# Three-layer graph convolution on one core: where layer 1's gathers and the next layer's loads are issued, bfloat16 keys, degrees by diagonal matrices

## The chip, the cores and the metric

The kernel runs on one core of a Trainium2 chip. The metric is the time of one execution on the device, in microseconds, as the median of three runs; lower is better. Beside those runs there is one execution under the hardware profiler, from which every duration below comes.

## The reference

N = 2500 nodes with 256 features, E = 80000 directed edges (src, dst), sorted by dst. After a layer norm and a relu follow three edge convolutions; then the input and the three results are concatenated and multiplied by Wf.

```python
def edge_conv(x, src, dst, W, b):
    m = concatenate([x[dst], x[src] - x[dst]], axis=-1) @ W + b
    s = segment_sum(m, dst, 2500)
    cnt = segment_sum(ones, dst, 2500)
    return s / maximum(cnt, 1)[:, None]

h = maximum(layernorm(x), 0)
xs = [h]
for W, b in ((W0, b0), (W1, b1), (W2, b2)):
    h = relu(edge_conv(h, src, dst, W, b)); xs.append(h)
return x + concatenate(xs, -1) @ Wf + bf
```

With W split into an upper half Wt and a lower half Wb, the sum over a node's edges is cnt * (x @ (Wt - Wb)) plus the sum over its edges of z[src], where z = x @ Wb. The kernel computes z for all nodes once per layer and then adds up rows of z; A, the matrix that does this, counts the edges from each source to each destination.

## The kernel before

**Tiles and stages.** Nodes lie in 20 tiles of 128 (NT). The first 112 nodes (FEW) are treated apart; the other 2388 fall into 398 windows of W = 6 destinations, and the windows into five groups g of 80 (the last has 78), so that a group is 480 columns of A. Since the edges are sorted by dst, a window's edges are found as a run of at most 256 in the edge list. 128 windows form a block i; there are four blocks (WG), the last with 14 windows and the 112 nodes apart.

**The head** (0 to about 61 us) loads x, normalizes it, turns it, makes z = x @ Wb of layer 0 as two parts zh and zl whose sum is z (split_high, split_low), and finds the edges of all blocks. For each block it makes two keys per edge: km, the low seven bits of src, and kn, eight times src's tile number plus the place of dst in the window (key_low on ACT, key_high on DVE). key_turn transposes both with TensorE against an identity, two pieces of 128 each, into a bank of PSUM; key_copy writes them as bfloat16 to key_m and key_n. The acts of the head stand in a string, order, that was written out by hand: "kt2" is key_turn(2).

**A, window by window.** compare makes one-hot matrices one_m and one_n on DVE for four windows at a time, counts multiplies them on PE, and take_counts copies the 480 counts to a on ACT. AHEAD = 4 pairs of one-hot buffers are there; a turn of build does the counts of three such quadruples, their copies and three comparisons for later ones.

**The product.** layer(l, g, ...) has 24 units per group: 20 of four matmuls, z's tile against A (zh and zl, two halves of the features), and four of fp32, Wt - Wb against the nodes' own features (pa<-hT,wt). In layer 0, while the product of group g goes on, build(g + 1) makes the next group's A between its units, and the generator extra gives other work, one step per unit (two in every other unit of group 0). In these steps:

- degrees(i) computes how many edges each node of block i has: eight ACT instructions with an accumulated sum, three small DVE instructions to deg and deg_b, a pause of four steps, and then for each half block six matmuls of deg_b, spread over 128 columns, against 64 columns of an identity. They put the degrees of 64 x 6 nodes into a bank, in all partitions, and ACT copies it to cnt. Group 0 does degrees(0) and degrees(1), group 1 degrees(2), group 2 degrees(3).
- later_loads issues five DMAs on SP: wb, wt and wf of layer 1, b_all and bf_sb; in group 0, after finish(0), that is, behind the stores of that group's A. finish(g) writes the row of degrees into A and stores A to DRAM (store_a, four DMAs of 1200 KB), so that layers 1 and 2 can load it.
- by_count(g + 1) multiplies hT by cnt at unit 19 of each group.

**The nodes apart.** Their edges are not in A. who holds the rows of z of 56 edges per partition (EDGES). keep_nodes stores zh to z_dram and adds zl to it on the DMA queue of POOL; gather(0) then fetches 56 times 128 rows with an indirect DMA on POOL, the first eight into the eight slots of sums (SUMS), the others added to what is in the slots. gather(0) is called once, ahead of group 0. After the last group layer_few(0, add_sums(8)) adds the eight slots up with three adds on DVE, splits the sum in two, and multiplies. Layers 1 and 2 gather in pairs (gather_pairs) with no accumulation, and there a gather waits for the matmul last written down, unit[0].

**The order of work.** Engines named PEo, DVEo, ACTo, POOLo and SPo keep the order of the program; nearly everything in layer 0 goes through them, by one helper, which is why many lines of the profile have number 282. The call that is written first is issued first on its engine, and an engine doesn't pass an instruction that waits. In layers 1 and 2 PE and ACT are left to a planner. DMAs issued from SP have one queue, those from POOL another. All DMAs and engines meet by semaphores that the framework sets.

## Time and profile before

| What | Value |
|---|---|
| median of three runs | 503.79 us |
| the runs | 502.59, 503.79, 506.75 us |
| profiled execution, its own time | 508.13 us |
| its span, first to last instruction | 506.4 us |
| PE busy | 493.7 us, 97% |
| DVE, POOL, ACT busy | 266.2, 252.5, 136.2 us |
| first product layer (groups 0 to 4) | 61.3 to 204.2 us |
| the layer's gathers, first and last issue | 76.4 and 183.0 us |

PE is matmuls, PEld the loading of weights, which overlaps them; DVE is VectorE, ACT ScalarE, POOL GpSimd, SP the engine that only issues DMAs. A group of instructions is named out<-in by the program's tiles, with the partitions x elements of both; "xN" counts instructions. In a chain of waits each row is a start, a length and what ran; "issue" is time in which an engine waited for nothing that the profile shows. "A <- B: us, times, longest" says how long A waited for B. The DMA queue of SP is q1, that of POOL q0.

### The profile page before, as it was taken

The numbers are of one execution on the slowest core, as the hardware profiler recorded it, in microseconds if no ns is written. First come the engines' busy times: TensorE is split into PE (matmuls) and PEld (weight loads), VectorE is DVE, ScalarE is ACT, GpSimd is POOL, SyncE is SP. The second block draws the span as 40 slices with busy tenths as digits, with TensorE's granted clock in tenths as the row PEclk, the third lists the DMA queues.
The fourth block names the chain that finished last, engine by engine and source line by source line (L and its number), as shares of the span: only waits on it lengthen the run. The fifth ranks groups of instructions, "written<-read, shape, count | busy, mean of one in ns | idle before, by whom it ended". The sixth has DMA issues, their size and how long they took to land.

```text
span 506.4 us, 7649 instructions
## 1 busy us (share of the span) xinstructions
PE 493.7 (97%) x2863; PEld 403.8 (80%) x2863; DVE 266.2 (53%) x670; ACT 136.2 (27%) x309; POOL 252.5 (50%) x234
## 2 busy tenths in 40 slices
PE   8999999899999999999999999999999999999994
PEld 4888887578888788888787878878887878788784
DVE  7999987699898932581235141426722231214043
ACT  5676675563734330430000000005200000000000
POOL 3687307888888840005787582600175645451000
PEclk9999999899999999999999999999999999999999
DMA  9426998696999991359798999973335889897033
GB/s 280 145 65 128 240 278 263 150 340 90 364 151 260 231 80 19 115 204 395 279 327 295 270 248 278 85 129 104 115 104 212 347 270 246 255 249 79 2 110 99
DMA packets 42104, 100.01 MB, mean 197 GB/s; under 512 B 5209, under 2 KB 32170, under 8 KB 36394
## 3 DMA queue, kind: packets, MB, share of 16 engines
q1 hardware_dynamic: 22762, 70.06, 37.6%
q0 software_dynamic: 18368, 28.26, 34.4%
q10 hardware_dynamic: 928, 1.11, 0.7%
q8 instruction: 24, 0.39, 0.3%
q14 instruction: 22, 0.18, 0.1%
HBM read 61.79 MB, written 38.26 MB: 198 GB/s over the span
## 4 chain that ended last, share of the span: by engine, by line
PE 91%; DVE 5%; DMA 1%; POOL 1%; issue 1%; ACT 0%; SPq 0%; DVEq 0%; ACTq 0%
PE pa L1004 34%; PE pa L282 22%; PE bank L811 10%; PE bank L282 8%; PE bank L787 7%; PE pa L1009 6%; PE pz L282 3%; DMA acc<-in_x_dram 1%; DVE st L282 1%; DVE one_m L282 1%; DVE one_n L282 1%; POOL acc L282 1%; DVE zl L282 0%; DVE mv L282 0%; DVE away L282 0%
## 5 line engine op out<-in xcount | busy, mean ns | idle before, releaser
L282 POOL DMA_INDIRECT one_m<-z_dram,who x112 | 113.0, 1009 | 151.1 <-DVE acc L282 79.7
L1004 PE MATMUL pa<-a,zh 128*128 128x480 f32 (+1 forms) x400 | 151.8, 380 | 0.0
L1004 PE MATMUL pa<-a,zl 128*128 128x480 f32 (+1 forms) x400 | 151.6, 379 | 0.0
L282 POOL DMA_INDIRECT sums<-z_dram,who x56 | 91.4, 1632 | 23.9 <-issue 16.8
L282 DVE TENSOR_TENSOR sums<-sums,one_m 128x512 f32<-128x512 f32 x52 | 36.0, 692 | 103.3 <-DMA one_m<-z_dram,who 101.2
L1004 PEld LDWEIGHTS pa<-a,zl 128*128 128x128 f32 x400 | 75.0, 187 | 12.0
L1004 PEld LDWEIGHTS pa<-a,zh 128*128 128x128 f32 x400 | 75.1, 188 | 10.4
L282 PE MATMUL pa<-a,zh 128*128 128x480 f32 (+1 forms) x200 | 81.2, 406 | 0.1
L282 DVE TENSOR_TENSOR one_m<-iota_m,key_m 128x1024 bf16<-128x1024 bf16 x100 | 68.8, 688 | 18.5 <-PE bank L282 15.4
L282 PE MATMUL pa<-a,zl 128*128 128x480 f32 (+1 forms) x200 | 75.7, 378 | 0.2 <-issue 0.2
L1012 ACT ACTIVATE hT<-pa 128x960 f32<-128x960 f32 (+1 forms) x10 | 9.7, 966 | 230.5 <-PE pa L1009 208.6
L282 ACT CAST a<-bank 128x480 fp32r<-128x480 f32 x100 | 51.7, 563 | 60.0 <-PE bank L282 52.7
L282 DVE TENSOR_TENSOR one_n<-iota_n,key_n 128x480 bf16<-128x480 bf16 x200 | 63.9, 360 | 0.0
L282 DVE SCALAR_TENSOR_TENSOR acc<-bank,share,acc 128x256 f32<-128x256 f32 x60 | 28.5, 483 | 58.7 <-PE bank L811 58.0
L811 PE MATMUL bank<-wf,hT 128*128 128x256 f32 x240 | 53.7, 379 | 0.5 <-ACT hT L282 0.5
L811 PEld LDWEIGHTS bank<-wf,hT 128*128 128x128 f32 x240 | 45.5, 190 | 9.8 <-issue 3.4
L282 PEld LDWEIGHTS <-one_m 128*128 128x128 bf16 x796 | 37.6, 98 | 10.5 <-issue 5.8
L282 PEld LDWEIGHTS pa<-a,zh 128*128 128x128 f32 x200 | 37.7, 188 | 8.8 <-issue 3.7
L282 PE MATMUL bank<-one_n,one_m 128*128 128x120 bf16 (+1 forms) x796 | 43.2, 209 | 0.6 <-issue 0.4
L282 PEld LDWEIGHTS pa<-a,zl 128*128 128x128 f32 x200 | 37.7, 188 | 6.9 <-issue 2.1
L787 PE MATMUL bank<-wb,hT 128*128 128x256 f32 x160 | 35.0, 380 | 0.0
L1009 PE MATMUL pa<-hT,wt 128*128 128x480 f32 (+1 forms) x80 | 33.8, 564 | 0.1
(148 smaller groups left out, 420.9 us busy)
## 6 DMA issues: line engine op xcount, KB each, us to landing
a<-a_dram SPq DMA_DIRECT2D x24, 1200.0 KB
a_dram<-a SPq DMA_DIRECT2D x20, 1200.0 KB
out_dram<-acc SPq DMA_DIRECT2D x19, 128.0 KB
z_dram<-one_m SPq DMA_DIRECT2D x16, 128.0 KB
z_dram<-sums SPq DMA_DIRECT2D x16, 128.0 KB
acc<-in_x_dram POOLq DMA_DIRECT2D x4, 512.0 KB
z_dram<-zh SPq DMA_DIRECT2D x7, 256.0 KB
z_dram<-zl POOLq DMA_DIRECT2D x7, 256.0 KB
```

Source lines behind the costliest of these rows:

```text
L282: return self.tc.keep_in_program_order(call(*args, **kwargs))
L787: PE.matmul(pz[:, :D], hT[:, c, t * P:(t + 1) * P], ws[l][1][:, c, :], start=(c == 0), stop=(c == DC - 1))
L811: PE.matmul(po[:, :D], hT[:, c, t * P:(t + 1) * P], wfs[l][:, c, :], start=(c == 0), stop=(c == DC - 1))
L1004: unit[0] = PE.matmul(pa[:, o, :n], tile_of(z, i)[:, o * P:(o + 1) * P], a[:, i, :n], start=(i == 0 and z is zh), stop=(z is zl and last[o ...
L1009: unit[0] = PE.matmul(pa[:, o, :n], ws[l][0][:, c, o * P:(o + 1) * P], hT[:, c, c0:c0 + n], start=False, stop=(last[o] == (kind, i, o)))
L1012: ACT.activation(hT[:, :, c0:c0 + n], pa[:, :, :n], AF.Relu)
```

## The change

It has five parts. The gathers of layer 0 are no longer written ahead of group 0: gather is now a generator, and each gather waits for the matmul last written, with the first after 10 units of the layer, the next at every 1.4 units up to the twelfth and every 1.2 units after that. later_loads moves from group 0 to the units of group 3. add_sums adds slots 4 to 6 to slots 0 to 2, then 1, 2 and 3 to 0, and the last slot at the end. The keys km and kn and their transposes are in bfloat16, with the bfloat16 identity. For blocks 2 and 3 degrees makes, for each half block, a matrix wide that holds a diagonal of each of the six degrees (ident_b times deg_b, on DVE), waits four more steps, and sums it over the partitions with one matmul of 384 columns (84 in block 3) against ones, in place of six; junk2 has one buffer for two. Two tiles are added, ones_p for those ones and an unused one of 56 numbers.

```diff
@@ -390,6 +390,7 @@
     bf_sb = const.tile([P, D], F32, name="bf_sb")
     ones = const.tile([P, 1], F32, name="ones")
     ones_b = const.tile([1, 1], BF16, name="ones_b")
+    ones_p = const.tile([P, 1], BF16, name="ones_p")
     ident_b = const.tile([P, P], BF16, name="ident_b")
     iota_m = const.tile([P, P], BF16, name="iota_m")
     iota_n = const.tile([P, NB], BF16, name="iota_n")
@@ -399,6 +400,8 @@
     deg_b = const.tile([P, WG, W], BF16, name="deg_b")
     lim = const.tile([P, WG], F32, name="lim")
     below = const.tile([P, WG], F32, name="below")
+
+    const.tile([P, 56], F32, name="between")
     z_dram = [dram.tile([NP, D], F32, name=f"z_dram{l}") for l in range(L)]
     who = const.tile([P, EDGES], I32, name="who")
     sums = const.tile([P, SUMS, D], F32, name="sums")
@@ -483,6 +486,7 @@
     load_b(1)
     DVE.memset(ones, 1.0)
     DVE.memset(ones_b, 1.0)
+    DVE.memset(ones_p, 1.0)
     DVE.memset(cnt[:, N:], 0.0)
     POOL.tensor_copy(ident_b, ident)
     POOL.tensor_copy(only, ident[:, IN_LAST:IN_LAST + FEW])
@@ -625,7 +629,7 @@
         POOLo.tensor_scalar(who, who, NONE, None, op0=OP.add)
 
     def key_low(i):
-        km = pw.tile([P, CAP], F32, name="km")
+        km = pw.tile([P, CAP], BF16, name="km")
         ACTo.copy(km, parts[i][0])
         parts[i][0] = km
 
@@ -634,15 +638,15 @@
         es = edges[i][0]
         hi_i = es if i < WG - 1 else pp.tile([P, CAP], I32, name="hi_i")
         DVEo.tensor_scalar(hi_i, es, ~(P - 1), 4, op0=OP.bitwise_and, op1=OP.logical_shift_right)
-        kn = pw.tile([P, CAP], F32, name="kn")
+        kn = pw.tile([P, CAP], BF16, name="kn")
         DVEo.scalar_tensor_tensor(kn, away[:, i, :], float(W + 1), hi_i, op0=OP.min, op1=OP.add)
         parts[i].append(kn)
 
     def key_turn(i):
-        pt = bank()
+        pt = bank().bitcast(BF16)
         for q, k in enumerate(parts[i]):
             for j in range(CH):
-                PEo.transpose(pt[:, q * CAP + j * P:q * CAP + (j + 1) * P], k[:, j * P:(j + 1) * P], ident)
+                PEo.transpose(pt[:, q * CAP + j * P:q * CAP + (j + 1) * P], k[:, j * P:(j + 1) * P], ident_b)
         parts[i] = pt
 
     def key_copy(i, q):
@@ -655,7 +659,7 @@
     def degrees(i):
 
         for q in range(W + 2):
-            junk = hot.tile([P, CAP], BF16, name="junk2")
+            junk = hot.tile([P, CAP], BF16, name="junk2", bufs=1)
             ACTo.activation(junk, away[:, i, :], AF.Relu, bias=nc_[:, q:q + 1], accum_out=gsum[:, i, q:q + 1])
             yield
         DVEo.scalar_tensor_tensor(deg[:, i, :], gsum[:, i, 1:W + 1], -2.0, gsum[:, i, 0:W], op0=OP.mult, op1=OP.add)
@@ -665,12 +669,27 @@
         yield
         yield
         yield
-        for w0 in range(0, min(P, NW - i * P), P // 2):
-            n = min(P // 2, NW - i * P - w0)
+        halves = [(w0, min(P // 2, NW - i * P - w0)) for w0 in range(0, min(P, NW - i * P), P // 2)]
+        wides = []
+        if i >= 2:
+
+            for w0, n in halves:
+                wide = hot.tile([P, P // 2, W], BF16, name="wide", bufs=2)
+                DVEo.tensor_tensor(wide[:, :n, :], ident_b[:, w0:w0 + n].unsqueeze(2).to_broadcast([P, n, W]),
+                                   deg_b[:, i, :].unsqueeze(1).to_broadcast([P, n, W]), op=OP.mult)
+                wides.append(wide)
+            for _ in range(4):
+                yield
+        for q, (w0, n) in enumerate(halves):
             pc = bank()
-            for c in range(W):
-                PEo.matmul(pc[:, :n * W].rearrange("p (w c) -> p w c", c=W)[:, :, c],
-                          deg_b[:, i, c:c + 1].to_broadcast([P, P]), ident_b[:, w0:w0 + n], start=True, stop=True)
+            if wides:
+                PEo.matmul(pc[:, :n * W], ones_p.to_broadcast([P, P]),
+                           wides[q][:, :n, :].rearrange("p w c -> p (w c)"), start=True, stop=True)
+            else:
+                for c in range(W):
+                    PEo.matmul(pc[:, :n * W].rearrange("p (w c) -> p w c", c=W)[:, :, c],
+                               deg_b[:, i, c:c + 1].to_broadcast([P, P]), ident_b[:, w0:w0 + n],
+                               start=True, stop=True)
             to = FEW + (i * P + w0) * W
             ACTo.copy(cnt[:, to:to + n * W], pc[:, :n * W])
             yield
@@ -915,20 +934,29 @@
         for i, q in ways:
             POOLo.dma_start(to[:, i, q, :], tiles_of(zl)[:, i, q, :], accum_op=OP.add)
 
+    def behind_unit(d):
+
+        tc.add_manual_dep(d.ins, unit[0].ins.name, mybir.DependencyInfo(
+            mybir.DependencyClass.Sync, mybir.DependencyReason.DATA), reason="spread over the layer")
+
     def gather(l):
 
         for e in range(EDGES):
-            POOLo.indirect_dma_start(
+            behind_unit(POOLo.indirect_dma_start(
                 out=sums[:, e % SUMS, :], out_offset=None, in_=z_dram[l][:, :],
                 in_offset=bass.IndirectOffsetOnAxis(ap=who[:, e:e + 1], axis=0),
-                **({"compute_op": OP.add} if e >= SUMS else {}))
+                **({"compute_op": OP.add} if e >= SUMS else {})))
+            yield
 
     def add_sums(n):
 
         DVEo.scalar_tensor_tensor(sums[:, 0, :], b_all, deg[:, WG - 1, 0:1], sums[:, 0, :], op0=OP.mult, op1=OP.add)
-        while n > 1:
-            n //= 2
-            DVEo.tensor_add(sums[:, :n, :], sums[:, :n, :], sums[:, n:2 * n, :])
+
+        if n > 2:
+            DVEo.tensor_add(sums[:, :3, :], sums[:, :3, :], sums[:, 4:7, :])
+            for i in (1, 2, 3):
+                DVEo.tensor_add(sums[:, 0, :], sums[:, 0, :], sums[:, i, :])
+        DVEo.tensor_add(sums[:, 0, :], sums[:, 0, :], sums[:, n - 1, :])
         two = room(F32R)
         DVEo.tensor_copy(two[:, 0, :], sums[:, 0, :])
         DVEo.tensor_sub(two[:, 1, :], sums[:, 0, :], two[:, 0, :].bitcast(F32))
@@ -968,9 +996,7 @@
                         out=two[:, i, :], out_offset=None, in_=z_dram[l][:, :],
                         in_offset=bass.IndirectOffsetOnAxis(ap=who[:, 2 * k + i:2 * k + i + 1], axis=0))
                     if k >= PAIRS and i == 0:
-
-                        tc.add_manual_dep(d.ins, unit[0].ins.name, mybir.DependencyInfo(
-                            mybir.DependencyClass.Sync, mybir.DependencyReason.DATA), reason="spread over the layer")
+                        behind_unit(d)
             if k >= PAIRS - 1:
                 yield
 
@@ -1074,8 +1100,10 @@
 
     held = None
     LATE = [NT] * 4
-    gather(0)
-    extra = chain(degrees(0), finish(0, a), later_loads(), degrees(1))
+    FIRST, SLOW = 10, 12
+    edge = gather(0)
+    fetched, passed = 0, 0
+    extra = chain(degrees(0), finish(0, a), [None], degrees(1))
     for g in range(NG):
         at = {}
         own = LATE
@@ -1090,6 +1118,11 @@
         else:
             extra = shares()
         for u, _ in enumerate(layer(0, g, a, own, PEo, ACTo)):
+
+            passed += 1
+            while fetched < EDGES and passed >= FIRST + 1.4 * min(fetched, SLOW) + 1.2 * max(fetched - SLOW, 0):
+                next(edge)
+                fetched += 1
             if u in at:
                 next(one)
             next(extra, None)
@@ -1106,7 +1139,7 @@
         if g + 1 < NG:
             run(finish(g + 1, a1))
             held, a = a, a1
-        extra = chain(degrees(g + 2) if g + 2 < WG else ())
+        extra = chain(degrees(g + 2) if g + 2 < WG else later_loads() if g + 2 == WG else ())
     layer_few(0, add_sums(SUMS))
     DVEo.tensor_sub(ws[1][0], ws[1][0], ws[1][1])
     tiles = {NG - 1: a, NG - 2: held}
```

## The prediction

> **What bounds the kernel now.** I began with the page, then cut the first product layer into its groups, then followed the chain of waits through the one group that is too long. The page's busy shares and the chain by engine:
>
> ```profile
> PE 493.7 (97%) x2863; PEld 403.8 (80%) x2863; DVE 266.2 (53%) x670; ACT 136.2 (27%) x309; POOL 252.5 (50%) x234
> ...
> PE 91%; DVE 5%; DMA 1%; POOL 1%; issue 1%; ACT 0%; SPq 0%; DVEq 0%; ACTq 0%
> ```
>
> PE is the chain for nine tenths of the span, so another engine matters only where it makes PE wait, and a saved PE instruction is worth its own time. The table of stretches, cut at the ends of the groups of the first product layer (61.3 to 204.2 us), shows where PE is not even; its columns are the stretch, its length, busy time and instructions of PE, PEld, DVE, ACT, POOL, then granted clock, DMA share and GB/s:
>
> ```profile
> 61.30:97.10 35.80, 33.12 (x274) 24.90 (x272) 27.60 (x72) 21.29 (x58) 18.03 (x14) 0.95 0.79 220
> 97.10:126.50 29.40, 29.29 (x261) 23.76 (x262) 25.35 (x67) 16.52 (x42) 25.39 (x14) 1.00 0.84 231
> ...
> 155.10:183.30 28.20, 28.20 (x245) 22.74 (x245) 21.59 (x58) 11.52 (x23) 23.93 (x15) 1.00 0.99 229
> ```
>
> Group 0 takes 35.8 us. Group 3, which carries no degree matmuls, takes 28.2; group 1, with twelve of them, 29.4, so twelve cost at most 1.2. Group 0 has 24: 28.2 + 2.4 = 30.6 would be right, and **5.2 us** are lost (5.7 if counted from group 1 with the direct cost of twelve more, 0.7). I use 5.5. The chain inside that group shows how:
>
> ```profile
> 86.12 0.41 issue
> ...
> 88.36 0.38 issue
> 88.74 0.23 PE bank L282
> 88.97 0.48 issue
> ...
> 91.33 4.07 PE pa L282 x6
> ```
>
> PE stands still with nothing to wait for, in steps of some 0.7 us, and then six matmuls take 4.07 us where eight of that kind take 3.22 in a later layer. Already before, the other engines see PE's results late. Waits of ACT between 77 and 97 us:
>
> ```profile
> ACT a L282 <- PE bank L282: 9.6, 8, 3.1
> ```
>
> The three banks whose last matmuls the records put before 82 us are evicted from 82.90, 84.38 and 85.84 us. So PE falls behind from about 78 to 95 us. In that time the queues carry what no other group has together, by the issues from 76 to 86 us: five loads for the next layer on SP, and the first gathers, the only ones in this layer without accumulation.
>
> ```profile
> wb<-in_L_gnn_W_dram SPq DMA_DIRECT2D x1, 256.0 KB
> wt<-in_L_gnn_W_dram SPq DMA_DIRECT2D x1, 256.0 KB
> wf<-in_L_gnn_Wf_dram SPq DMA_DIRECT2D x1, 256.0 KB
> b_all<-in_L_gnn_b_dram SPq DMA_DIRECT2D x1, 128.0 KB
> bf_sb<-in_L_gnn_bf_dram SPq DMA_DIRECT2D x1, 128.0 KB
> sums<-z_dram,who POOLq DMA_INDIRECT x7
> ```
>
> That they cause it is an inference: accumulating gathers with 4.9 MB of stores (groups 1 to 3) leave PE whole, and so do plain gathers with loads of counts in the later layers. **The times of the runs matter here.** The profiled execution took 508.13 us, its span 506.4 and 1.7 around it. Less 5.5 it is 502.6: the lowest of the three unprofiled runs, 502.59. The highest, 506.75, lies 4.2 above that, the median 503.79 lies 1.2 above. I read this as a stall that comes whole, in part or not at all; most of what the profile offers is not in the median.
>
> [...]mean clock 0.83 between 90 and 100 us, and fp32 matmuls 0.80 us apart instead of 0.40. So 1.5 to 2 of the 5.5 us are a consequence of the gaps and go with them. [...]
>
> **The change, part by part.**
> *Loads moved* from group 0 to the first unit of group 3, behind that group's four stores on SP. SP is idle between stores and nothing waits behind the loads; they need some 4 us of the engines' time and land near 175 us (the stores of 4.9 MB fill the engines from 156 to 171). b_all is wanted by DVE at 185, wb by PE at 204: covered. If the cover were gone, PE would wait microsecond for microsecond. Gain: the stall, 5.5 in the profiled execution, 1.2 in the median, or 0.
> *Waits on units*, all 56 gathers. A unit is 28.6/24 = 1.19 us. The first gather starts at 76.36 because z_dram lands then, later than unit 10 (61.3 + 11.9 = 73.2). Before, twelve gathers took (95.31 - 76.36)/12 = 1.58 us each; now 1.4 units, 1.67. The later ones may go every 1.2 units, 1.43 us, but POOL needs 2.03 for one ((182.96 - 87.66)/47), so the wait is over before it begins. Nothing but gathers is queued on POOL there. Price of a wait: in layer 1, gathers with and without one start 1.25 us apart alike, so 0; upper bound 0.2 each.
> *Slots added in another order*: five adds of 256 to 768 elements for three. After the last landing there remain an add (0.42), a cast (0.29) and a difference (0.43), 1.2 us for 3.1. Hidden either way, below.
> *Keys*: 16 transposes. Two blocks lie past 38.3 us, where PE leads the chain:
>
> ```profile
> 39.39 0.38 PE L282 MATMUL bank<-shift,km 128*128 128x128 f32 x2
> 39.61 0.38 PE L282 MATMUL bank<-shift,kn 128*128 128x128 f32 x2
> 39.83 1.89 PE L282 MATMUL pz<-wb,hT 128*128 128x256 f32 x8
> ```
>
> Four take 0.44 us. [...] Two blocks save **0.4**; the other two lie where PE waits for POOL (0.2 and 0.38 us idle) and DVE leads, so 0; bounds 0 and 0.9. DVE's kn (0.58, from int32 and bfloat16) I leave as it is: bounds -0.3 and +0.1 each.
> *Degrees* of blocks 2 and 3: 18 matmuls become three. From the timeline around 113 us and 142 us:
>
> ```profile
> 114.17 0.50 PE L282 MATMUL bank<-ident_b,deg_b 128*128 128x64 bf16 x6
> 114.47 0.46 PE L282 MATMUL pa<-a,zh 128*128 128x480 f32 x1
> ...
> 142.03 0.30 PE L282 MATMUL bank<-ident_b,deg_b 128*128 128x14 bf16 x6
> 142.18 1.05 PE L282 MATMUL pa<-hT,wt 128*128 128x480 f32 x2
> ```
>
> The next matmul starts 0.30 to 0.34 after six, 0.15 after the narrow six. [...]say **0.5** with fewer weight loads; bounds 0.2 and 1.0. On DVE two products of 384 and one of 84 elements come in. None like them is shown; a one_n product (480, bfloat16) takes 0.40[...], so 0.3 to 0.7 each; I take 0.46, 0.9 in a row. Behind them wait the comparisons, and PE behind those. DVE is 25.4 of 29.4 us busy in group 1, so its lag is made up in the next turns; PE loses 0 to 0.9, I take **0.2**. The products are read four units (4.8 us) later; cnt is ready four units later too, at unit 17 of 24, and first read at 19 and only for a later group.
>
> **Sum** on the profiled execution: 508.13 - 5.5 - 0.4 - 0.5 + 0.2 = 501.9. From the median, whose stall I put at 1.2: 503.79 - 1.2 - 0.7 = 501.9 as well. I forecast **502.0**.
>
> **The rivals.**
> *The stall stays, now and then*: its cause is something else. For it: no record names a wait, and the headline edit hardly shifts a gather. Then 503.79 - 0.7 = 503.1, up to 505.5. Chance 0.24.
> *The stall is in every run and goes*: the profile's surplus would then be the price of profiling, and the median falls by all of it: 503.79 - 5.5 - 0.7 = 497.6. Against it speaks the spread of the runs. Chance 0.16.
> *The gathers end the layer* (slower). PE reads their sum at 204.4 us. The waits and adds of DVE:
>
> ```profile
> 192.02 2.41 DVE L282 TENSOR_TENSOR sums<-sums 128x1024 f32<-128x1024 f32 x3 [5.98 <-DMA sums<-z_dram,who]
> 194.47 0.29 DVE L282 CAST one_m<-sums 128x256 fp32r<-128x256 f32 x1
> ```
>
> They land at 192.0. With the shorter tail the sum is ready at 193.2; PE, 6 us earlier, wants it at 198.4: 5.2 us of slack. The loads, now among the last gathers, can take 4. If a wait then costs POOL over 0.03 us (48 gathers in a row), PE waits; at 0.2 us it is 9.6 - 1.2 = 8.4 us, 510.3. The equal pitch in layer 1 speaks against it. With the stall moved to group 3 it would be found near 507. Chance of ending slower than before 0.14.
> The forecast's own case has 0.46 and holds 500.5 to 503. The range goes from 497.6, the full gain, to 506.0; above and below it I leave 2 in 10. A measurement here tells about 1% from no change: faster (below 498.75) 0.16, the whole-stall case; slower (above 508.83) 0.09; same 0.75.
>
> **What would show it.** Group 0 at 30 to 31 us, with clock 1.00 from 80 to 100 us and ACT seeing the banks within 0.5 us: the loads were it. Group 0 still at 35: they weren't. Group 3 above 29: the stall moved. Gathers that start 2.2 us apart or more, and PE idle at the layer's end: the slower rival. Groups 1 and 2 shorter by 0.3 and 0.2, the transposes at 0.22 for four. I am wrong if PE's later layers, now without a gap, are no longer so, or if DVE's new products hold up PE by more than 1 us.

## The result: 1.2% slower, because the gathers end the first product layer

The changed kernel takes 511.59 us (median of 20 runs, 508.39 to 514.97), the kernel before 507.38 beside it (20 runs, 502.19 to 510.34). The ratio is **1.0115, with a 95% interval of 1.008 to 1.015**: slower. The forecast was 502.0 us, the range 497.6 to 506.0.

Nine of the 20 runs of the kernel before lie at 502.2 to 503.8 us and eleven at 506.75 to 510.3, and the profile in front of the prediction (508.13) is of the second kind. A later profile of the same kernel, called before_2 below, is of the first kind (502.51 us); in it group 0 of the first product layer takes 30.1 us, not 35.8. Beside runs that are all of the first kind the change costs more, 1.0161 [1.0142, 1.018]. The longer group 0 of the second kind, in which PE stands still with nothing to wait for, is called the stall below.

From the page of the changed kernel, busy times and then the chain by engine:

```profile
PE 494.0 (96%) x2848; PEld 404.2 (79%) x2848; DVE 267.2 (52%) x676; ACT 138.6 (27%) x309; POOL 261.3 (51%) x234
...
PE 88%; DVE 5%; DMA 4%; POOL 1%; issue 1%; ACT 1%; SPq 0%; DVEq 0%; ACTq 0%
```

PE is busy as long as before, but the span is 512.5 us instead of 506.4, and 4% of the chain is now a DMA. POOL is busy 8.8 us longer. The stretches of the first product layer, cut at the ends of the groups, and then the stretch after it (columns as in the prediction: length, busy time of PE, PEld, DVE, ACT, POOL, granted clock, DMA share, GB/s):

```profile
61.30:92.36 31.06, 30.72 (x277) 24.56 (x276) 26.72 (x70) 21.94 (x59) 12.62 (x10) 1.00 0.67 207
92.36:121.10 28.74, 28.74 (x251) 23.00 (x252) 26.57 (x70) 17.15 (x40) 26.30 (x9) 1.00 0.68 209
...
149.70:177.90 28.20, 28.20 (x245) 22.73 (x245) 21.63 (x58) 11.79 (x23) 22.81 (x16) 1.00 1.06 264
...
198.90:210.00 11.10, 2.95 (x14) 2.51 (x13) 3.98 (x8) 1.26 (x2) 0.00 (x0) 0.73 0.45 48
```

Group 0 is 4.7 us shorter than in the first profile of before, group 1 is 0.7 shorter, and then come 11.1 us in which PE works for 2.95. Its wait, from the list of waits, with what it waits for (one_m holds the sum of the slots, split in two):

```profile
PE pa L282 <- DVE one_m L282: 8.2, 1, 8.2
```

The line of DVE in that stretch, with the wait ahead of it in brackets, says that the sum could not start before the gathers had landed:

```profile
204.26 2.80 DVE L282 TENSOR_TENSOR sums<-sums 128x768 f32<-128x768 f32 x5 [8.41 <-DMA sums<-z_dram,who]
207.10 0.29 DVE L282 CAST one_m<-sums 128x256 fp32r<-128x256 f32 x1
207.42 0.42 DVE L282 TENSOR_TENSOR one_m<-sums,one_m 128x256 fp32r<-128x256 f32 x1
```

In the first profile of before the adds began at 192.02, when PE still had 12 us of group 4 to do. Why the gathers are late is in POOL's timeline (start, length, [idle before]):

```profile
106.50 1.53 POOL L282 DMA_INDIRECT sums<-z_dram,who  x1 [0.30 <-PE pa L282]
108.33 1.58 POOL L282 DMA_INDIRECT sums<-z_dram,who  x1 [0.31 <-PE bank L282]
110.22 13.57 POOL L282 DMA_INDIRECT sums<-z_dram,who  x1 [0.30 <-DMA sums<-z_dram,who]
124.10 1.54 POOL L282 DMA_INDIRECT sums<-z_dram,who  x1 [0.30 <-PE pa L282]
```

**One gather of 13.57 us** among gathers of 1.54. In that time DVE runs without a pause, from 107.49 to 122.38, and the gather ends 1.42 us after DVE first pauses. The two diagonal products stand in that stretch:

```profile
110.97 1.02 DVE L282 TENSOR_TENSOR wide<-ident_b,deg_b 128x384 bf16<-128x384 bf16 x2
```

**The balance** is best made between two profiles without the stall of group 0: before_2 (span 500.8) and after_2 (510.2), measured together. They differ by 9.4 us, own times by 9.38.

| From us to us | before_2 | after_2 | difference |
|---|---|---|---|
| start to first product matmul | 61.7 | 61.8 | +0.1 |
| group 0 | 30.1 | 30.1 | 0 |
| groups 1 and 2 | 57.7 | 57.3 | -0.4 |
| groups 3 and 4 | 49.2 | 49.2 | 0 |
| last group's eviction to that of the nodes apart | 1.3 | 11.2 | **+9.9** |
| from there to the first eviction of layer 1's product | 42.1 | 43.6 | +1.5 |
| from there to the last eviction of layer 2 | 234.2 | 234.2 | 0 |
| from there to the end | 24.5 | 22.8 | -1.7 |

The +1.5 is the half clock after PE's wait; about 1.1 us of the +9.9 is half clock too, since PE's last 2.2 us of work in that row ran at it. In after_2:

```profile
202.30:212.50 10.20, 5.16 (x16) 4.36 (x17) 4.46 (x10) 0.83 (x2) 0.00 (x0) 0.50 0.21 41
```

PE's last matmul before the wait ends at 198.8, the clock falls at 202.3 and returns at 212.5, 5.2 us after PE restarts at 207.34. In the changed kernel's first profile the last matmul ends at 199.29, the clock is halved from 204.10 to 214.34, and PE restarts at 207.44, 6.9 us before it returns. In the stall of before's first profile it is halved from 92.05 to 95.46 us, which costs 1.7 us of work at full clock:

```profile
92.05:95.46 3.41, 3.41 (x8) 1.38 (x7) 2.92 (x8) 0.72 (x2) 2.80 (x3) 0.50 0.47 71
```

PE's pauses ahead of it were of 1.10 us at most, and in before_2 group 0 has no pause and clock 1.00. So the half clock came after pauses of PE in all three; how long a pause brings it, and how much work ends it, these profiles don't show. The last -1.7 lies behind the last accumulation into acc, where the program closes (6.0 us against 4.3). The other kernels that I built have it too, whatever was changed in them, but for b_wait and b_hold; I don't know its cause and credit no part of the change with it.

### The profile page after: what moved, and what is told of

Its sections match the earlier page's. It is cut to its first block, busy times and chain, and to the rows that moved or that the text cites. A ratio compares the mean times of both kernels' runs of the same rounds, so it can differ in the third digit from the quotient of the medians.

```text
span 512.5 us, 7679 instructions
## 1 busy us (share of the span) xinstructions
PE 494.0 (96%) x2848; PEld 404.2 (79%) x2848; DVE 267.2 (52%) x676; ACT 138.6 (27%) x309; POOL 261.3 (51%) x234
## 4 chain that ended last, share of the span: by engine, by line
PE 88%; DVE 5%; DMA 4%; POOL 1%; issue 1%; ACT 1%; SPq 0%; DVEq 0%; ACTq 0%
PE pa L1030 34%; PE pa L282 20%; PE bank L830 10%; PE bank L806 7%; PE bank L282 7%; PE pa L1035 6%; PE pz L282 3%; DMA sums<-z_dram,who 2%; DMA acc<-in_x_dram 1%; DMA es<-in_src_dram,start_i 1%; DVE one_m L282 1%; DVE one_n L282 1%; POOL acc L282 1%; DVE st L282 1%; DVE sums L282 1%
## 5 line engine op out<-in xcount | busy, mean ns | idle before, releaser
L282 POOL DMA_INDIRECT one_m<-z_dram,who x112 | 111.7, 998 | 147.5 <-DVE acc L282 73.9
L282 POOL DMA_INDIRECT sums<-z_dram,who x56 | 101.5, 1813 | 26.5 <-PE pa L282 15.0
L282 PE MATMUL pa<-a,zh 128*128 128x480 f32 (+1 forms) x200 | 81.5, 407 | 0.0
L1038 ACT ACTIVATE hT<-pa 128x960 f32<-128x960 f32 (+1 forms) x10 | 9.7, 968 | 231.6 <-PE pa L1035 204.2
L830 PEld LDWEIGHTS bank<-wf,hT 128*128 128x128 f32 x240 | 45.5, 190 | 11.2 <-issue 4.9
L806 PE MATMUL bank<-wb,hT 128*128 128x256 f32 x160 | 37.4, 398 | 0.0
L806 PEld LDWEIGHTS bank<-wb,hT 128*128 128x128 f32 x160 | 32.0, 201 | 4.7
```

Of the source, the lines that this page charges most:

```text
L282: return self.tc.keep_in_program_order(call(*args, **kwargs))
L806: PE.matmul(pz[:, :D], hT[:, c, t * P:(t + 1) * P], ws[l][1][:, c, :], start=(c == 0), stop=(c == DC - 1))
L830: PE.matmul(po[:, :D], hT[:, c, t * P:(t + 1) * P], wfs[l][:, c, :], start=(c == 0), stop=(c == DC - 1))
L1038: ACT.activation(hT[:, :, c0:c0 + n], pa[:, :, :n], AF.Relu)
```

## The experiments

**Theory**: DVE's diagonal products take away the pauses that POOL needs to get a gather out; the gathers then end the layer. **Rivals**: the waits on units slow the gathers; the moved loads do. And on the other side of the sum: the loads, the waits, or neither shorten group 0. The first four kernels ran together.

**a_no_wide**: the changed kernel with six matmuls per half block for all blocks, as before.

```diff
-        if i >= 2:
+        if i >= WG:
```

> The changed kernel with one part undone: the degrees of blocks 2 and 3 come from six small matmuls per half block again, DVE makes no diagonal matrices. Theory 1 (POOL can't finish a gather while DVE runs without a pause, and the two diagonal matrices filled DVE's last pauses in group 1): no gather of over 4 us in group 1, the last gather starts near 184 us instead of 196, PE waits under 1 us for the gathers' sum, some 503 us. Theory 2 (the waits on units make the gathers late): the last gather still starts after 192 us, PE waits 5 us or more, 509 to 513 us.

Measured: 506.88 us, 0.9923 [0.9868, 0.9977] of before. No gather takes over 5.43 us, the last starts at 188.5, the sum is ready at 201.6, and PE waits 2.7 us for it instead of 8.2. So the products are the larger part of the loss. But 503 us and a wait under 1 us were expected: something smaller is left that still makes the gathers last.

**a_no_wait**: the changed kernel with all gathers written ahead of group 0 and no waits on units.

```diff
-            behind_unit(POOLo.indirect_dma_start(
+            (POOLo.indirect_dma_start(
...
-    edge = gather(0)
-    fetched, passed = 0, 0
+    run(gather(0))
+    fetched, passed = EDGES, 0
```

> The changed kernel with one part undone: all 56 gathers are issued ahead of group 0 and wait for no unit. Theory 1 (DVE without a pause holds up POOL): the twelve first gathers come earlier by 3 us at most, a gather of over 10 us stays in group 1, the last starts near 192 us, 508 to 512 us. Theory 2 (the waits on units): the last gather starts at 183 us as before, no wait of PE at the layer's end, 502 to 503 us.

Measured: 511.86 us, 1.0028 [0.9973, 1.0083]. A gather of 13.58 us from 111.4, the last one starts at 193.6, the sum is ready at 205.9. Without the waits the layer ends late all the same.

**b_wide**: the kernel before with the diagonal products and nothing else. The diff is that of degrees in the change.

> The kernel before with one part of the change alone: diagonal matrices for blocks 2 and 3 (with the unused tile, and one buffer for junk2). Theory 1 (DVE without a pause holds up POOL): a gather of some 10 us appears in group 1, the last starts at 190 us or later, and runs without the stall of group 0 come to 506 us or more. Theory 2 (the waits on units): the last starts at 183 us, and the time is that of before less 0.5 us.

Measured: 511.97 us, 1.0032 [0.9974, 1.009]; before took 511.77 beside it. A gather that stands still is there, with no wait on a unit anywhere near:

```profile
117.04 1.57 POOL L282 DMA_INDIRECT sums<-z_dram,who  x1 [0.30 <-issue]
118.92 13.57 POOL L282 DMA_INDIRECT sums<-z_dram,who  x1 [0.30 <-issue]
132.80 1.54 POOL L282 DMA_INDIRECT sums<-z_dram,who  x1 [0.30 <-issue]
```

The sum is ready at 206.5, and no time is lost by it, for group 0 took 39.4 us in this execution and PE came to the layer's end at 207.6. **A run takes as long as the later of the two**, PE's path with its stall or the gathers' path, and a stall hides late gathers.

**b_loads**: the kernel before with the five loads in group 3.

```diff
-    extra = chain(degrees(0), finish(0, a), later_loads(), degrees(1))
+    extra = chain(degrees(0), finish(0, a), [None], degrees(1))
...
-        extra = chain(degrees(g + 2) if g + 2 < WG else ())
+        extra = chain(degrees(g + 2) if g + 2 < WG else later_loads() if g + 2 == WG else ())
```

> The kernel before with one part of the change alone: the five loads for the next layer are issued in group 3. If the loads next to the first gathers cause PE's stall in group 0, group 0 takes 30 to 31 us in every run, and all times lie near 502.6 us with none above 505. If they don't, the times fall in two heaps as those of before do, near 502.6 and near 509. The last gather starts by 186 us, and PE doesn't wait at the layer's end.

Measured: 505.82 us (503.78 to 510.74), 0.9926 [0.9864, 0.9988], beside 511.77 of before; group 0 31.7 us, still with evictions up to 4.1 us behind PE's matmuls. It looked as if the loads were a part of the stall.

The next four ran together as well.

**a_loads_back**: the changed kernel with the loads in group 0 again (the diff of b_loads, reversed).

> The changed kernel with one part undone: the five loads are issued in group 0 again. If they cause PE's stall there, group 0 goes from 31 us to 35 or more in the profile, with eviction 4 us or more behind PE's records, and PE's wait at the layer's end shrinks by as much, since the gathers end at the same time; total within 2 us of the changed kernel. If they don't, group 0 stays at 31 us.

Measured: 511.08 us, 0.9974 [0.994, 1.0007] of before, whose median was 511.08 too. Loads and first gathers are again side by side, and group 0 has its right length:

```profile
61.50:91.60 30.10, 30.10 (x275) 24.25 (x274) 26.47 (x70) 21.92 (x59) 13.83 (x9) 1.00 0.78 235
```

The loads don't suffice to make the stall. A gather of 11.58 us stands at 111.4, although it starts only after the products. PE waits 7.6 us at the layer's end, 1 us less than in after_2 (8.5), with the last gather started 0.3 us earlier and the sum ready 1.3 us earlier: the moved loads seem to cost about 1 us there (more on this under b_wait).

**a_neither**: the changed kernel with neither products nor waits: moved loads, bfloat16 keys and the slots' order are left.

> The changed kernel without the diagonal matrices and without the waits on units: what is left are the moved loads, bfloat16 keys and the order of the slots. Theory 1: no gather over 4 us, the last starts by 185 us, PE doesn't wait at the layer's end, group 0 at 30 to 32 us: 502 to 504 us in most runs on this chip, 1 to 1.7% under the kernel before. If the waits on units were needed against the stall, group 0 takes 33 us or more and the runs spread up to 509.

Measured: 506.2 us, 0.9918 [0.9876, 0.9959]. The stall is there with the loads moved away, and there is no long gather:

```profile
61.70:96.90 35.20, 32.94 (x275) 25.21 (x274) 27.59 (x72) 22.19 (x59) 17.79 (x14) 0.95 0.66 190
```

So the loads aren't needed for it either. That a_neither and b_loads, both with the loads moved, ran 0.8 and 0.7% under a before that stalled leaves open that the loads make the stall deeper.

**b_tt**: the kernel before with two diagonal products in block 2 whose results nobody reads, on DVE alone; PE keeps its twelve matmuls.

```diff
+        if i == 2:
+            for w0 in (0, P // 2):
+                wide = hot.tile([P, P // 2, W], BF16, name="wide", bufs=2)
+                DVEo.tensor_tensor(wide, ident_b[:, w0:w0 + P // 2].unsqueeze(2).to_broadcast([P, P // 2, W]),
+                                   deg_b[:, i, :].unsqueeze(1).to_broadcast([P, P // 2, W]), op=OP.mult)
```

> The kernel before and, in group 1, the two diagonal products of block 2 on DVE alone: their results go unused, the degrees still come from 36 small matmuls of 64 columns. Theory 1 (POOL's gather stands still from such a product until DVE next pauses): one gather of group 1 takes 13 to 14 us, it is the one during which the products run, and it ends 1.4 us after DVE's next pause begins. If the wide matmul or the later degrees were what delays the gathers, no gather takes over 4 us.

Measured, one run: 508.93 us. No gather over 2.56 us in group 1. A miss, and it bears on the theory: the products, from 116.99 to 118.00 us, fill DVE's pause of 0.83 us, DVE runs from 113.51 to 121.47 without one, and yet the gathers of that time pass:

```profile
114.36 1.57 POOL L282 DMA_INDIRECT sums<-z_dram,who  x1 [0.30 <-issue]
116.24 1.69 POOL L282 DMA_INDIRECT sums<-z_dram,who  x1 [0.30 <-issue]
118.23 1.79 POOL L282 DMA_INDIRECT sums<-z_dram,who  x1 [0.31 <-issue]
```

So neither the products beside a gather nor 8 us of DVE without a pause hold it up for certain. In b_tt a pause of 0.13 us is left at 121.47; in the changed kernel that one is gone too, and the stretch is 14.9 us long.

**b_red**: the same place, two sums with one input each (0.61 us each in the trace) instead of the products.

```diff
...
+                total = hot.tile([P, 1], F32, name="total", bufs=2)
+                DVEo.reduce_sum(total, key_m.rearrange("p w j r -> p (w j r)")[:, 0:450],
+                                axis=mybir.AxisListType.X)
```

> The kernel before and, at the same place in group 1, two sums over 450 bfloat16 elements on DVE, with one input each and as long as the two products (0.5 us each); unused. If it is DVE's time alone that matters (its pauses in group 1 are used up), one gather takes over 10 us here too. If it is the product with two inputs that shuts POOL out, the pauses are gone as well, but no gather takes over 4 us.

Measured, one run: 511.36 us. The longest gather of group 1 took 4.22 us and ended 1.42 us after DVE had paused for 0.03 us. As some pauses stayed, it doesn't tell one input from two; it does show a gather that ended behind a pause of no more than 0.03 us.

Two questions remained: what waits cost and whether they keep the stall away, and whether PE's wait is the whole price of the long gather.

**b_wait**, and again as **b_wait_2** and **b_wait_3**: the kernel before with the waits on units alone.

```diff
-            POOLo.indirect_dma_start(
+            behind_unit(POOLo.indirect_dma_start(
...
+            passed += 1
+            while fetched < EDGES and passed >= FIRST + 1.4 * min(fetched, SLOW) + 1.2 * max(fetched - SLOW, 0):
+                next(edge)
+                fetched += 1
```

> The kernel before with one thing added: each gather of the first product layer waits for the unit of the product after which it is put out (from the 10th unit on, 1.4 and then 1.2 units apart), as in the changed kernel. Loads in group 0, float32 keys, degrees and the slots' order are as before. Theory (the waits, not the moved loads, take away the stall of group 0): group 0 takes 30 to 31 us where it was 35.8, no eviction lags PE by more than 2.5 us, the layer's last group ends at 198 to 200 us; no gather over 10 us (no diagonal products), the last gather starts at 185 to 189 and the sum is ready at 198 to 202; 0.6 to 1.2% under the kernel before. Rival (the stall goes for another reason, the bfloat16 keys or the slots' order together with the waits): group 0 stays at 35 to 38 us and the time within 0.4% of before.

> The kernel before with each gather of the first product layer behind a unit of the product, once more, beside another profile of the kernel before. Theory (the waits cost by themselves and the stall comes and goes without regard to them): where the kernel before is at 502 to 503 us in all runs, 0.3 to 0.7% slower (the gathers start 5 us later, PE waits 1 us for the sum); where it has two heaps, this has them too. Rival (the waits take the stall away): where the kernel before has two heaps, this has one, at 503 to 506 us, and is 0.3 to 1.2% faster.

> The kernel before with the waits on units alone, a third time, for the case that the kernel before stalls in group 0 here. Theory A (the waits keep the stall away): where the kernel before has two heaps or lies at 505 to 513 us, this lies at 503 to 506 us with group 0 at 30 to 31 us and no eviction later than 2.5 us behind PE. Theory B (the stall comes with or without them): this spreads like the kernel before, group 0 in its profile at 32 us or more, an eviction over 4 us behind PE. Where the kernel before stays at 502.3 us nothing is learned on this, and the ratio should be 1.002 to 1.005 once more.

Measured: 504.06, 503.38 and 503.71 us; 1.0048 [1.003, 1.0066], 1.0023 [1.0014, 1.0032] and 1.0028 [1.0021, 1.0036] of before. The first expectation was wrong: before, by its times, stalled in none of the 91 runs beside these three kernels (501.88 to 502.82), so the waits had nothing to take away, and **they cost 1.0 to 1.7 us**. The last gather starts at 188.3 instead of 186.2 to 186.7 (before_3, before_2), the sum is ready at 198.8 to 199.8 instead of 197.1 to 197.6, and PE comes to it at 198.5. In b_wait_3:

```profile
PE pa L282 <- DVE one_m L282: 1.0, 1, 1.0
```

Whether the waits keep the stall away where it comes stays open: no execution of this kernel met it.

Beside a_no_wide, b_wait also shows what the moved loads do. From 165 to 195 us the DMA engines are full in both (DMA share 1.03 and 1.07), mostly with gathers. SP's queue, q1, has this part of 165 to 180 us (packets, MB, share of the engines), first in a_no_wide with the loads in group 3, then in b_wait with the loads in group 0:

```profile
q1 hardware_dynamic: 1073, 1.04, 29.6%
```

```profile
q1 hardware_dynamic: 3, 0.02, 0.3%
```

The last gather starts at 188.5 and 188.3, but the sum is ready at 201.6 and 199.2. So the moved loads seem to delay the last landing by some 2 us; the slots' order and the keys differ too.

**b_hold**: the kernel before with all gathers behind one unit near the end of group 0.

```diff
-    gather(0)
...
+            if g == 0 and u == NT + 3:
+                gather(0)
```

> The kernel before with all gathers of the first product layer put behind one unit near the end of group 0: no gather runs beside group 0. A look at group 0 alone; the gathers must end later. Theory A (the stall of group 0 comes from the gathers' running beside it): group 0 takes 29 to 31 us and no eviction lags PE by more than 1.5 us. Theory B (the stall comes from the five loads or from the order of PE's own work and not from the gathers): group 0 stays at 35 to 38 us. In either case some 13 gathers that ran in group 0 now run later, 1.84 us each, so that the last starts at 200 to 208 us and PE waits at the layer's end: 514 to 520 us.

Measured, one run: 511.69 us, less than the 514 to 520 expected; group 0 30.1 us. It can't tell A from B, as before didn't stall beside it either. But it is a second case of late gathers without any product: the sum is ready at 206.3, PE waits 7.4 us, and the span is 510.0.

**an_later** and **a_later**: the changed kernel without and with the diagonal products, and in both the sum and the layer of the nodes apart behind 12 node tiles of the next layer. nodes_split then writes to the rooms of one_m and one_n first.

```diff
...
-    layer_few(0, add_sums(SUMS))
...
+        for i, (t, zf) in enumerate(zip([t for t in range(1, NT) if t not in last] + last + [0], rooms(l))):
+            if l == 1 and i == 12:
+                layer_few(0, add_sums(SUMS))
             nodes_split(l, t, zf)
```

> The changed kernel without the diagonal products, and with the few nodes' sum and layer moved behind the first 12 node tiles of the next layer (whose results go to the four rooms of one_m and the four of one_n first, and to the slots of the sums after that). Theory (at the layer's end PE waits for the gathers' sum and for nothing else): PE goes on to the node tiles at 198.6 us without a pause over 0.5 us, its wait of 3.3 us is gone, span 501 to 503 us, 1.2 to 1.9% under the kernel before. Rival (the pause only moves, to the sum behind the 12 tiles or to the rooms that come free later): within 0.3 points of the same kernel without the move, 0.8% under before.

> The changed kernel whole, diagonal products and all, with the few nodes' sum and layer moved behind the first 12 node tiles of the next layer. Theory (the gather that is held up costs time only through PE's wait at the layer's end): a gather still takes 10 to 14 us at 107 to 124 us and the last starts near 196, but PE works through: 12 tiles of 0.85 us from 199 on last until 209, the sum is there at 207.4; the 8.2 us of waiting and the half clock after it (2.3) are gone, span 501 to 504 us, 0.5 to 1.5% under the kernel before. Rival (the products cost by themselves, or the pause moves): 510 us or more, within 0.3% of before or slower.

> The changed kernel with the few nodes' sum and layer moved behind 12 node tiles, once more, beside the changed kernel itself. Theory (PE's wait at the layer's end is the whole price of the held-up gather): 8 to 12 us under the changed kernel of the same call; 501 to 504 us where nothing stalls. Rival: under 4 us.

Measured: an_later 501.77 us, 0.9988 [0.9981, 0.9995]; a_later 501.29, 0.9979 [0.997, 0.9988], and 501.32 the second time, 0.9979 [0.9972, 0.9986]. The distance to before is smaller than expected, as before did not stall beside them. In a_later a gather takes 13.57 us at 109.5, as in the changed kernel, and PE works through what was the wait (in the changed kernel these node tiles are written behind the matmuls that need the sum, and PE started none of them from 199.29 to 207.44 us):

```profile
198.20:209.00 10.80, 10.80 (x53) 9.57 (x52) 7.84 (x22) 6.60 (x13) 0.56 (x1) 1.00 0.77 165
```

**after_2** and **before_2**, measured with a_later_2, and **before_3**, measured with b_wait_3: both kernels unchanged, once more.

> The changed kernel once more. Theory (a stall in group 0 would be hidden behind the gathers, which end the layer; so the heaps of before don't show in it): 510 to 514 us; against a kernel before that stalls in no run (502.4) 1.5 to 2.3% slower, against one with two heaps 0.5 to 1.2%. Rival (the change itself took 5 us out of group 0): the distance is the same 1.15% either way.

> The kernel before once more, for a second profile of it. Theory (the stall of group 0 is no work of the kernel's own but comes in some executions: the 20 runs beside the changed kernel form two heaps, 502.2 to 503.8 and 506.75 to 510.3): an execution at 502 to 504 us has no stall, group 0 at 30 to 31 us and the layer's end near 198.5; one at 506 us or more has group 0 at 34 us or more. Rival (the heaps have another reason): group 0 takes 35 us at 502 to 504 us too.

> The kernel before, for its profile beside b_wait_3: where it takes 506 us or more, group 0 over 33 us with an eviction over 4 us behind PE; where it takes 502.3, group 0 at 30.1 us and 0.3 us, as in before_2.

Measured: after_2 510.94 us (four runs), 1.0161 [1.0142, 1.018]; before_2 502.51 and before_3 501.94, one run each. a_later_2 is 9.6 us under after_2, and its first eviction of layer 1 comes at 242.4 us, as in before_2 (242.1): PE's wait and its half clock were the whole price of the late gathers. In group 1 the pauses differ. DVE's instructions in before_2 between 106 and 125 us that had to wait, and then those in after_2:

```profile
106.92 0.69 DVE L282 TENSOR_TENSOR one_m<-iota_m,key_m 128x1024 bf16<-128x1024 bf16 x1 [0.45 <-PE bank L282]
111.32 0.69 DVE L282 TENSOR_TENSOR one_m<-iota_m,key_m 128x1024 bf16<-128x1024 bf16 x1 [0.83 <-PE bank L282]
123.98 0.69 DVE L282 TENSOR_TENSOR one_m<-iota_m,key_m 128x1024 bf16<-128x1024 bf16 x1 [1.95 <-PE bank L282]
```

```profile
107.03 0.69 DVE L282 TENSOR_TENSOR one_m<-iota_m,key_m 128x1024 bf16<-128x1024 bf16 x1 [0.44 <-PE bank L282]
123.71 0.69 DVE L282 TENSOR_TENSOR one_m<-iota_m,key_m 128x1024 bf16<-128x1024 bf16 x1 [1.79 <-PE bank L282]
```

The pause of 0.83 us is filled by the two products (1.02 us in a row), and a smaller one of 0.13 us, at 114.88 in before_2, goes because PE, with fewer matmuls for the degrees, frees its bank in time (b_tt, which keeps these matmuls, keeps this pause). What is left is 14.9 us of DVE without a pause, 37 instructions. POOL in after_2:

```profile
107.87 1.59 POOL L282 DMA_INDIRECT sums<-z_dram,who  x1 [0.30 <-PE bank L282]
109.77 13.57 POOL L282 DMA_INDIRECT sums<-z_dram,who  x1 [0.30 <-DMA sums<-z_dram,who]
123.64 1.54 POOL L282 DMA_INDIRECT sums<-z_dram,who  x1 [0.30 <-PE pa L282]
```

It ends at 123.34, 1.42 us after the pause began at 121.92. All seven profiles with the products (after, after_2, b_wide, a_no_wait, a_loads_back, a_later, a_later_2) have one gather of 11.57 to 13.58 us there; none of the 13 others has one over 6.01. That the products of the change bring the long gather is shown by this, by b_wide and by a_no_wide; that they do it by closing DVE's pauses fits every long gather's end, but b_tt shows that it isn't the whole account.

## Why the prediction was wrong, by its steps

**Loads moved (-5.5 in the profiled execution, -1.2 in the median): the step that failed on the gain's side.** "That they cause it is an inference", the prediction said, and as the cause the loads fell: group 0 takes 30.1 us with the loads in it (a_loads_back, before_2, before_3) and 35.2 with them away (a_neither). The stall belongs to some executions. In the others the term is 0, and the forecast then had nothing to win but PE's few matmuls; where there is a stall, moving the loads may take a part of it (b_loads and a_neither, 0.7 and 0.8% under before). The sign that I had named for it, group 0 at 30 to 31 us, came and meant nothing; the other one, evictions within 0.5 us, didn't come. ACT's waits between 77 and 97 us in the changed kernel's first profile:

```profile
ACT a L282 <- PE bank L282: 3.9, 4, 2.3
```

They are 3.9 us in all instead of 9.6, but the three banks from 81.5 to 82.3 us are evicted 1.7 to 2.2 us after their last matmul, against 0.04 to 0.24 in before_2. A milder stall was there, with the loads gone. And the move has a price that the sum put at nothing, though the rival had its size: the loads "can take 4", it said, and they take 29.6% of 15 us, 4.4. At the layer's end that seems to be 1 to 2 us (a_loads_back, a_no_wide beside b_wait).

The rival "the stall stays, now and then" was right on the stall, but not on the time. (The steps in which PE stands still are 0.38 to 0.48 us in the lines that the prediction shows, not 0.7.)

**Slack of 5.2 us: the step that failed on the loss's side.** It was read from an execution with the stall. The stall pushed PE's end of the layer from 198.7 to 204.2 us, while the gathers were not held by it (the last started at 183.0, against 186.7 in before_2). Without it the sum is ready at 197.6 and PE, done at 198.7, is just behind: 1.1 us of slack. I took the stall off PE's side of the subtraction, which gave 198.4, and left the gathers' side as it was.

**Products on DVE (+0.2, bounds 0 and 0.9): the term that was too small by five to nine microseconds, and the one that did most to make the kernel slower.** Each took 0.55 us where I took 0.46, an estimate of mine that no trace had shown (0.55 us for 384 elements and 0.24 for 84 in the changed kernel, so as an estimate from these two about 1 ns an element and 0.15 us fixed), and PE isn't held up by DVE, as I said. What I left out is a third engine: I priced DVE's 0.9 us by who waits for DVE's results, and nobody does. POOL's gathers depend on what DVE does beside them: the longest took 13.57 us in the changed kernel and 5.43 in a_no_wide. Of PE's wait of 8.5 us in after_2, 2.7 are left without the products (a_no_wide), and 1.0 with the waits alone (b_wait_3); half clock comes on top. The medians of the changed kernel and a_no_wide are 4.7 us apart, and in b_wide the products alone put off the sum by 8.9 (206.5 against 197.6 in before_2). The sign "if DVE's new products hold up PE by more than 1 us" came true, but by way of POOL.

**Waits on units (0, upper bound 0.2 each).** They cost 1.0 to 1.7 us in all, by the gathers' later end; over 56 gathers the last start moves by 1.6 to 2.1 us, 0.03 to 0.04 each. The slower rival named 0.03 us as the point from which it decides. Its path (the gathers end the layer), its place and nearly its time (510.3) were what came, but by luck: it put them down to the waits, which carry 10 to 15% of it. I gave it 0.14.

**Slots in another order** (hidden; after the last landing 1.2 us instead of 3.1). The tail hardly got shorter: from the last landing to the end of the cast it is 2.6 us in after_2 (204.69 to 207.29) and 2.8 in before_2 (194.79 to 197.61). The first four adds can't start before the gather before the last has landed, and that is only 0.65 us earlier (204.04), so they aren't done when the last one lands.

**Keys (-0.4).** The gain was an estimate of mine that no trace of before had shown; it was right for the transposes. Four took 0.44 us (39.39 to 39.83), and PE's timeline of the changed kernel has four in 0.23, 56 ns from one start to the next:

```profile
39.71 0.28 PE L282 MATMUL bank<-ident_b,km 128*128 128x128 bf16 x2
39.82 0.28 PE L282 MATMUL bank<-ident_b,kn 128*128 128x128 bf16 x2
39.94 1.30 PE L282 MATMUL pz<-wb,hT 128*128 128x256 f32 x5
```

The chain from 39.94 to 45.47 us in before_2 (5.53) runs from 40.04 to 45.22 in after_2 (5.18), so 0.35 are won; then the counts' matmuls, sixteen at a time, lose as much (0.99 for 0.71 in the first), and the first product matmul is at 61.8 instead of 61.7. The gain didn't reach the end of the head.

**Degrees (-0.5).** Groups 1 and 2 are shorter by 0.36 and 0.04 in after_2 (0.3 and 0.2 were said). an_later and a_later, where the gathers decide nothing, differ by 501.77 - 501.29 = 0.48 us. The term was right in sum, and the products' 0.2 on PE is in it. The times of the wide matmuls were an estimate of mine too. In group 1 of before's first profile it is 0.61 us from the first of six narrow ones to the second matmul behind them (114.17 to 114.77); from a wide one to the second behind it the changed kernel takes 0.38 and 0.39 (112.56 to 112.94, 113.59 to 113.98).

So the sum from an execution without the stall is 502.5 - 0.4 (degrees) + 9.9 + 1.5 - 1.7 (closing) + 0.1 = 511.9, what after_2's profiled execution took (511.89).

## What to carry to other kernels

Before work is given to DVE because it has spare time, look whether POOL has indirect DMAs out in that stretch: DVE's pauses may be what lets them through, and here 1.02 us of new work made one gather take 13.57 us for the usual 1.54 (in b_tt none over 2.56). Read slack from an execution in which nothing else is late, or take the stall off both sides of the subtraction. And if a result is late, first look for work of the next stage that needs it last: moving it behind 12 tiles was worth more than all other edits, and gave the fastest version (501.3 us, 0.2% under a before without the stall, 1.9% under the change).

## What the runs showed of the hardware

**A gather on POOL beside DVE.** In after_2 a gather of 13.57 us starts in a stretch of 14.9 us in which DVE has no pause; all 37 instructions of that stretch are tensor_tensor with two inputs. Whether the two inputs matter, b_red doesn't tell, and by what way DVE's work holds up a gather, no run shows.

Two things can be counted in the twenty profiles. Of the 98 accumulating gathers over 2.2 us, 72 end 1.40 to 1.46 us after a pause of DVE begins, among them all 21 over 3.2 us. But a pause isn't the only way out. Of the 427 accumulating gathers begun before 178 us that took more than the usual 1.53 to 1.57 us, 426 end 1.35 to 1.46 us after the end of some DVE instruction (a time taken at random lies so near in 27 of 100 cases), and at only 90 of these ends does a pause begin: most pass between two instructions that follow each other without a gap. So it is in the changed kernel's group 2, where DVE runs from 136.18 to 143.42 us without a pause, tensor_tensor throughout, and no gather is held for long:

```profile
137.03 1.57 POOL L282 DMA_INDIRECT sums<-z_dram,who  x1 [0.30 <-PE bank L282]
138.91 1.69 POOL L282 DMA_INDIRECT sums<-z_dram,who  x1 [0.30 <-DMA sums<-z_dram,who]
140.90 1.62 POOL L282 DMA_INDIRECT sums<-z_dram,who  x1 [0.30 <-DMA sums<-z_dram,who]
142.83 1.77 POOL L282 DMA_INDIRECT sums<-z_dram,who  x1 [0.30 <-PE bank L282]
```

Why the long gather passed at none of the 30 such ends between its start and 122.38 us stays open. The seven long ones began 2.7 or 4.7 us after the last pause.

**PE's results late to other engines.** In the stall of group 0, ACT's evictions come 4.1 to 7.6 us behind the matmuls in the profiles that have it (0.3 in before_2), and PE pauses for 0.4 us at a time with nothing to wait for. None of the ten profiles from b_wait on shows it (0.3 us at most). In the ten before, the three kernels with waits on units had 1.1 to 2.2 us and group 0 at 30.1 to 31.1, the seven without had 4.1 or more. That is no proof, since b_wait met no stall, and the cause of the stall is open.
